# Context halves and three projection weights on one load queue, turned on TensorE in the order of landing, both context copies on VectorE

## The chip, the cores and the metric

One Trainium2 chip, of which the kernel uses one core. The metric is the device time of one execution in microseconds (us). Before the change three runs took 472.63, 471.83 and 472.56 us; the median is 472.56.

## What is computed

Eight sequences `x` of 512 tokens with 256 features are refined with a context of 64 rows per sequence. Cut to what matters:

```python
nx = layer_norm(x, ln_gamma, ln_beta)            # (8, 512, 256)
q = nx @ Wq
k, v = context @ Wk, context @ Wv                # context: (8, 64, 256)
weights = softmax(q @ k.T * 256 ** -0.5)
evidence = weights @ v
combined = concat([nx, evidence, broadcast(cond)])
router_probs = softmax(combined @ router_W + router_b)          # 3 experts
h = silu(combined @ e_w1 + e_b1)                                # 768 -> 512 per expert
routed = sum(router_probs * (h @ e_w2 + e_b2))
g = sigmoid(silu(combined @ gate_w1 + gate_b1) @ gate_w2 + gate_b2)
out = x + g * (routed @ out_w + out_b)
```

All of it is in float32.

## The kernel before, in words

The kernel has a setup stage and then a loop over four pairs of sequences (`NP = B // 2`, from L1138). In the loop the gate, the three experts and the outputs are computed with TensorE products of 128 x 128 weights by 128 x 512 tokens (`product`, L675). Setup and loop are written with `tc.manual_schedule(engines=None)`: each engine runs its instructions in the order in which the program lists them, and an instruction waits on semaphores for what it reads and for buffers that it overwrites. Nothing is planned by a cost model.

The change lies in the setup stage, in its first eight microseconds or so. That stage prepares what the attention needs from the context:

- *Loads.* L1078 to L1092 issue the large loads. The context is seen as 512 rows, in `NX = 4` tiles of 128 rows, and comes in two halves of 256 KB (`ctx_sb`, L1081). `Wk` and `Wq` (256 KB each, L1083) are issued by ScalarE (ACT). `Wv` (L1084), two sequences of x (512 KB each, `load_x`, L126) and the gate's and experts' first weights (`load_first`, `load_anchor`, L191 to L196) are issued by SyncE (SP). The queue that SP uses is called q1 in the profile, the one that ACT uses q10. GpSimd (POOL) issues small loads of bias rows (L172 to L179) in its own queue.
- *Wake products.* `wake(n)` (L250) lists n TensorE products of a tile of zeros with itself. Their result is never read.
- *Transposes.* The products with the context need it with features on the partitions. `context_transposes` (L271) takes a half at a time: four TensorE transposes of 128 x 128 into one PSUM bank, then one copy of 128 x 512 to `ctxT` in SBUF. The first half's copy is VectorE's (DVE), the second half's ScalarE's (L284). A `wake(1)` lies between the halves. `transpose_weights` (L286) does the same for a weight: four transposes into a bank and a copy on ScalarE (L293). It is called for Wk and for Wq.
- *Products.* `project` (L295) with Wv gives `vT` in two halves (`ps_v`, copied by ScalarE, L305), `join_keys` (L307) multiplies the turned Wk and Wq (`ps_kq`) so that keys and queries need one product, and `project` with that result gives `mr` (`ps_m`, copied by VectorE, L319).
- *PSUM banks.* `either` (L244) hands out four banks in turn for these steps.
- *The first two sequences.* `statistics` (L457) on VectorE computes mean and variance of each token of x as soon as x has landed; `deviation` (ScalarE), `normalize` (VectorE) and `transpose_x` (TensorE, copies on ScalarE and VectorE) follow, then `scores` and `softmax`.

The order on TensorE from the start is: 7 wake products, transposes of the first half, 1 wake product, transposes of the second half, of Wk, of Wq, half of the Wv products (`ps_v`), `join_keys`, the other half of Wv.

```python
        wake(7)
        context_transposes()
        transpose_weights(wkT, wk_sb, "wk")
        transpose_weights(wqT, wq_sb, "wq")
        statistics(0, 0, NT)
        deviation(0, 0)
        normalize(0)
        project(wv_sb, ctxT, keep_v, "v", (0,))
        join_keys()
```

Of the kernel before, what the change touches and what calls it, by code (L numbers as in the profile page):

```python
# [16 lines left out]
def kernel(  # L17
# [50 lines left out]
    nc = tc.nc  # L68
    P = 128
# [3 lines left out]
    KH = H // P  # L73
# [23 lines left out]
    def bank(i, name):  # L97
        return psum.tile([P, 512], F32, tag=f"b{i}", name=name)
# [4 lines left out]
    def misc(name):  # L103
        spare.append(spare.pop(0))
        return bank(spare[-1], name)
# [6 lines left out]
    ident = const.tile([P, P], F32, tag="ident", name="ident")  # L112
# [19 lines left out]
    def rows_of(w):  # L132
        return w.rearrange("(k p) n -> p k n", p=P)


    NX = B * CT // P
# [5 lines left out]
    def by_k(flat, n):  # L142
        return flat.rearrange("p (k n) -> p k n", n=n)

    scr = scratch(1, 2, "scr_ctx")
    ctx_sb, ctxT = by_k(scr[:, :HK], H), by_k(scr[:, HK:], B * CT)
    scr = scratch(1, 1, "scr_w")
    wk_sb, wq_sb, wqT, wv_sb = (by_k(scr[:, i * KH * H : (i + 1) * KH * H], H) for i in range(4))
# [95 lines left out]
    def either(name):  # L244
        turn[0] += 1
        return bank((1, 2, 0, 3)[turn[0] % 4], name)
# [3 lines left out]
    def wake(n):  # L250

        if not ps_wake:
            ps_wake.append(misc("ps_wake"))
        for _ in range(n):
            nc.tensor.matmul(ps_wake[0][:, :P], zeros, zeros, start=True, stop=True)  # L255
# [12 lines left out]
            condT[:, :, :B], pt[:, : KH * B].rearrange("p (k b) -> p k b", b=B)  # L268
        )

    def context_transposes():  # L271
        for d in range(2):
            if d:
                wake(1)
            pt = either(f"pt_ctx_{d}").rearrange("p (k c) -> p k c", k=KH)
            for k in range(KH):
                for t in range(NX // 2):
                    nc.tensor.transpose(
                        pt[:, k, t * P : (t + 1) * P],
                        ctx_sb[:, d * (NX // 2) + t, k * P : (k + 1) * P],  # L280
                        ident,
                    )
            half = slice(d * NX // 2 * P, (d + 1) * NX // 2 * P)
            (nc.scalar.copy if d else nc.vector.tensor_copy)(ctxT[:, :, half], pt)  # L284

    def transpose_weights(dst, w_sb, name):  # L286
        pt = either(f"pt_{name}")
        for k in range(KH):
            for i in range(KH):
                nc.tensor.transpose(  # L290
                    pt[:, k * H + i * P : k * H + (i + 1) * P], w_sb[:, i, k * P : (k + 1) * P], ident
                )
        nc.scalar.copy(dst.rearrange("p k n -> p (k n)"), pt)  # L293
# [163 lines left out]
    def statistics(b, t0, t1):  # L457
        j, i = b // 2, b % 2
        if b % 2 == 0 and t0 == 0:
            S["mv", j] = work.tile([P, 2, NT, nc.vector.BN_AGGR_DIM], F32, tag="mv", name=f"mv_{j}")  # L460
            S["sd", j] = work.tile([P, 2, NT], F32, tag="sd", name=f"sd_{j}")
        for t in range(t0, t1):
            st = work.tile([P, nc.vector.BN_STATS_DIM], F32, tag="st", name=f"st_{b}_{t}")
            nc.vector.bn_stats(st, x_sb[b][:, t, :])
            nc.vector.bn_aggr(S["mv", j][:, i, t, :], st)
# [610 lines left out]

    with tc.manual_schedule(engines=None):
        ctx_rows = context.flatten_outer_dims().rearrange("(t p) d -> p t d", p=P)  # L1078
        for d in range(2):
            half = slice(d * NX // 2, (d + 1) * NX // 2)  # L1080
            nc.sync.dma_start(ctx_sb[:, half, :], ctx_rows[:, half, :])  # L1081
        for w_sb, w in ((wk_sb, Wk), (wq_sb, Wq)):
            nc.scalar.dma_start(w_sb, rows_of(w))  # L1083
        nc.sync.dma_start(wv_sb, rows_of(Wv))  # L1084
        load_table(AF.Sqrt)
        load_x(0)
# [4 lines left out]
        for g in (1, 2):  # L1091
            load_first(g)  # L1092

        wake(7)
        context_transposes()
        transpose_weights(wkT, wk_sb, "wk")
        transpose_weights(wqT, wq_sb, "wq")
        statistics(0, 0, NT)
        deviation(0, 0)
# [148 lines left out]
```

## Time and profile before

| what | value |
|---|---|
| median of three runs | 472.56 us |
| the profiled execution, its own time | 472.56 us |
| span of the profiled execution, from first to last instruction | 470.4 us |
| TensorE (PE) busy | 465.1 us, 99% of the span |
| TensorE weight loads (PEld), overlapping PE | 221.1 us, 47% |
| VectorE (DVE) busy | 353.8 us, 75% |
| ScalarE (ACT) busy | 215.4 us, 46% |
| GpSimd (POOL) busy | 85.1 us, 18% |
| moved by the DMA engines | 36.84 MB, 78 GB/s over the span |

How to read it: the profile is one execution of the program, taken by the hardware profiler. Times count from the start of the span in microseconds. A group of instructions is named by its line in the kernel, its engine, its operation, and the tile that it writes and those that it reads (`out<-in`). PE's records overlap, since products are pipelined: a record's length is not what the product costs in a stream, the distance to the next record's start is. A wake product of float32 has two records, a transpose one. The chain of waits is followed back from the last instruction; in it each piece counts only what lies after the end of the piece before. For a load the profile gives the time from its issue to the landing of its last byte. "issue" in brackets is idle time for which the profile shows no other engine's work.

### The profile page before, as it was taken

The numbers are of one execution on the slowest core, as the hardware profiler recorded it, in microseconds if no ns is written. First come the engines' busy times: TensorE is split into PE (matmuls) and PEld (weight loads), VectorE is DVE, ScalarE is ACT, GpSimd is POOL, SyncE is SP. The second block draws the span as 40 slices with busy tenths as digits, with TensorE's granted clock in tenths as the row PEclk, the third lists the DMA queues.
The fourth block names the chain that finished last, engine by engine and source line by source line (L and its number), as shares of the span: only waits on it lengthen the run. The fifth ranks groups of instructions, "written<-read, shape, count | busy, mean of one in ns | idle before, by whom it ended". The sixth has DMA issues, their size and how long they took to land.

```text
span 470.4 us, 4664 instructions
## 1 busy us (share of the span) xinstructions
PE 465.1 (99%) x1439; PEld 221.1 (47%) x1439; DVE 353.8 (75%) x653; ACT 215.4 (46%) x388; POOL 85.1 (18%) x111
## 2 busy tenths in 40 slices
PE   9999999999999999999999999999999999999996
PEld 7744546445444444445454444445454444444454
DVE  3755847989989555889989555898989624797972
ACT  3455565657211647657311546658311465457000
POOL 5318123200062300000062300000052400000020
PEclk9999999999999999999999999999999999999999
DMA  9968330056232830442122740352122560000013
GB/s 288 376 108 179 57 136 0 0 117 90 36 67 32 171 135 0 91 88 45 17 47 44 162 152 1 75 106 45 18 45 45 84 186 0 1 0 1 0 22 68
DMA packets 126424, 36.84 MB, mean 78 GB/s; under 512 B 111548, under 2 KB 123392, under 8 KB 125888
## 3 DMA queue, kind: packets, MB, share of 16 engines
q1 hardware_dynamic: 122656, 28.59, 29.1%
q0 software_dynamic: 1856, 7.18, 4.8%
q10 hardware_dynamic: 1888, 0.79, 0.6%
q8 instruction: 11, 0.18, 0.2%
q14 instruction: 13, 0.11, 0.1%
HBM read 28.36 MB, written 8.18 MB: 78 GB/s over the span
## 4 chain that ended last, share of the span: by engine, by line
PE 91%; DVE 4%; SPq 3%; DMA 0%; issue 0%; ACT 0%; ACTq 0%
PE ps_u L677 40%; PE ps_z L677 17%; PE ps_y L677 14%; PE ps_vw L652 4%; SPq L392 3%; PE ps_gu L677 3%; PE ps_s L537 3%; PE ps_w2o L418 2%; PE ps_gz L677 1%; DVE h L951 1%; PE ps_wake L255 1%; DVE h L760 1%; PE ps_m L299 1%; PE ps_v L299 1%; PE ps_gy L677 1%; DVE r L960 0%
## 5 line engine op out<-in xcount | busy, mean ns | idle before, releaser
L760 DVE TENSOR_TENSOR h<-h,pb 128x512 f32<-128x512 f32 x96 | 61.9, 693 | 10.5 <-ACT h L710 10.5
L677 PE MATMUL ps_u<-h,w2o 128*128 128x512 f32 x144 | 63.9, 593 | 0.0
L677 PE MATMUL ps_u<-nxT,w 128*128 128x512 f32 x112 | 55.6, 607 | 0.0
L710 ACT ACTIVATE h<-h,abias 128x512 f32<-128x512 f32 x72 | 49.2, 718 | 8.8 <-DVE h L716 8.2
L677 PE MATMUL ps_z<-wT,vw 64*128 64x512 f32 x104 | 49.5, 605 | 0.0
L983 POOL TENSOR_TENSOR yb<-yb,xb 128x512 f32<-128x512 f32 x14 | 19.1, 1368 | 150.1 <-DVE yb L982 144.7
L677 PE MATMUL ps_z<-h,w2s 128*128 128x512 f32 x96 | 42.8, 595 | 0.2 <-DVE r L966 0.2
L719 ACT COPY h<-ps_u 128x512 f32<-128x512 f32 x48 | 27.9, 582 | 32.2 <-PE ps_u L677 31.9
L677 PEld LDWEIGHTS ps_u<-h,w2o 128*128 128x128 f32 x144 | 27.1, 190 | 31.3 <-issue 29.4
L716 DVE TENSOR_TENSOR h<-h,ps_y 128x512 f32<-128x512 f32 x24 | 16.4, 683 | 28.9 <-PE ps_y L677 25.0
L951 DVE TENSOR_TENSOR h<-h,h 128x1024 f32<-128x1024 f32 x24 | 34.3, 1483 | 0.0
L677 PEld LDWEIGHTS ps_u<-nxT,w 128*128 128x128 f32 x112 | 19.9, 189 | 29.8 <-issue 24.9
L710 ACT ACTIVATE h<-ps_u,abias 128x512 f32<-128x512 f32 x24 | 16.5, 687 | 30.2 <-PE ps_z L677 30.2
L677 PE MATMUL ps_y<-nxT,w 128*128 128x512 f32 x56 | 28.6, 592 | 0.0
L677 PE MATMUL ps_z<-T,ws 128*128 128x512 f32 x56 | 28.6, 592 | 0.0
L677 PEld LDWEIGHTS ps_z<-h,w2s 128*128 128x128 f32 x96 | 17.9, 190 | 22.1 <-issue 21.1
L677 PE MATMUL ps_u<-wT,vw 64*128 64x512 f32 x56 | 27.8, 611 | 0.0
L338 POOL DMA_DIRECT2D vrd<-vw x4 | 3.2, 802 | 132.5 <-ACT vw L659 132.5
L677 PE MATMUL ps_y<-wT,vw 64*128 64x512 f32 x56 | 27.0, 596 | 0.0
L652 PE MATMUL ps_vw<-w,vT 128*128 128x512 f32 (+1 forms) x64 | 26.9, 541 | 0.0
L677 PE MATMUL ps_u<-T,ws 128*128 128x512 f32 x56 | 26.7, 594 | 0.0
L677 PE MATMUL ps_z<-nxT,ws 128*128 128x512 f32 x56 | 26.6, 592 | 0.0
(209 smaller groups left out, 790.2 us busy)
## 6 DMA issues: line engine op xcount, KB each, us to landing
pb<-pd POOLq DMA_DIRECT2D x4, 1536.0 KB, 7.7
x<-in_x_dram SPq DMA_DIRECT2D x8, 512.0 KB, 5.4
xb<-in_x_dram SPq DMA_DIRECT2D x64, 64.0 KB, 2.4
out_dram<-yb SPq DMA_DIRECT2D x56, 64.0 KB, 2.0
w<-in_L_xcond_e_w_dram SPq DMA_DIRECT2D x6, 512.0 KB, 9.5
xd<-x SPq DMA_DIRECT2D x6, 512.0 KB, 2.9
xg<-xd SPq DMA_DIRECT2D x48, 64.0 KB, 2.4
scr_wa<-in_L_xcond_e_w_dram SPq DMA_DIRECT2D x3, 512.0 KB, 10.2
```

Source lines behind the costliest of these rows:

```text
L299: nc.tensor.matmul(ps, w_sb[:, k, m * P : (m + 1) * P], src[:, k, :], start=(k == 0), stop=(k == KH - 1))
L392: nc.sync.dma_start(dst[i * TB : (i + 1) * TB, k, :].rearrange("r (j c) -> r j c", c=TB), src[:, lo : lo + TB].rearrange("(j r) c -> r j c ...
L418: nc.tensor.matmul(ps[:, d * H : (d + 1) * H], w2T[:, k, (i + d) * P : (i + d + 1) * P], ow_sb[:, k, :], start=(k == 0), stop=(k == KH - 1),)
L537: nc.tensor.matmul(ps[:, t, :], nxT[:, k, t * P : (t + 1) * P], mr[:, k, b, :], start=(k == 0), stop=(k == KH - 1),)
L652: nc.tensor.matmul(ps, vT[:, k, j * 2 * CT : (j + 1) * 2 * CT], w1[:, KH + k, n0:n1], start=(k == 0), stop=(k == KH - 1),)
L677: nc.tensor.matmul(ps, lhsT, rhs, start=start, stop=True, skip_group_check=not start)
L710: nc.scalar.activation(h, h if src is None else src, AF.Silu, bias=abias[:, c, 2 * j + i : 2 * j + i + 1])
L716: nc.vector.tensor_tensor(h, h, part, ALU.add)
L719: nc.scalar.copy(chunk(n, i, d), part)
L760: nc.vector.tensor_tensor(h, h, S["pb", j][:, i, 2 * q // RC, :], ALU.mult)
L951: nc.vector.tensor_tensor(d, p, m, ALU.subtract)
L983: nc.gpsimd.tensor_tensor(yb, yb, S["xb", 2 * j + row][:, i, :], ALU.add)
```

## The change

The five loads of 256 KB go into SP's queue in the order first half, Wk, second half, Wq, Wv; ACT issues no load here. The function for the context's transposes takes one half at a time and its copy is always VectorE's. TensorE's order becomes: 5 wake products, first half, Wk, 1 wake product, second half, Wq, then the Wv products as before. All other code stays.

```diff
-    def context_transposes():
-        for d in range(2):
-            if d:
-                wake(1)
-            pt = either(f"pt_ctx_{d}").rearrange("p (k c) -> p k c", k=KH)
-            for k in range(KH):
-                for t in range(NX // 2):
-                    nc.tensor.transpose(
-                        pt[:, k, t * P : (t + 1) * P],
-                        ctx_sb[:, d * (NX // 2) + t, k * P : (k + 1) * P],
-                        ident,
-                    )
-            half = slice(d * NX // 2 * P, (d + 1) * NX // 2 * P)
-            (nc.scalar.copy if d else nc.vector.tensor_copy)(ctxT[:, :, half], pt)
+    def transpose_context(d):
+        pt = either(f"pt_ctx_{d}").rearrange("p (k c) -> p k c", k=KH)
+        for k in range(KH):
+            for t in range(NX // 2):
+                nc.tensor.transpose(
+                    pt[:, k, t * P : (t + 1) * P],
+                    ctx_sb[:, d * (NX // 2) + t, k * P : (k + 1) * P],
+                    ident,
+                )
+        nc.vector.tensor_copy(ctxT[:, :, d * NX // 2 * P : (d + 1) * NX // 2 * P], pt)
...
         ctx_rows = context.flatten_outer_dims().rearrange("(t p) d -> p t d", p=P)
-        for d in range(2):
-            half = slice(d * NX // 2, (d + 1) * NX // 2)
-            nc.sync.dma_start(ctx_sb[:, half, :], ctx_rows[:, half, :])
-        for w_sb, w in ((wk_sb, Wk), (wq_sb, Wq)):
-            nc.scalar.dma_start(w_sb, rows_of(w))
+        for d, w_sb, w in ((0, wk_sb, Wk), (1, wq_sb, Wq)):
+            part = slice(d * NX // 2, (d + 1) * NX // 2)
+            nc.sync.dma_start(ctx_sb[:, part, :], ctx_rows[:, part, :])
+            nc.sync.dma_start(w_sb, rows_of(w))
         nc.sync.dma_start(wv_sb, rows_of(Wv))
...
-        wake(7)
-        context_transposes()
+        wake(5)
+        transpose_context(0)
         transpose_weights(wkT, wk_sb, "wk")
+        wake(1)
+        transpose_context(1)
         transpose_weights(wqT, wq_sb, "wq")
```

## The prediction, made before the changed kernel ran

> **What bounds the kernel now.** I read the page's first part, then the chain of waits up to 26 us, the timeline engine by engine up to 20 us, the landings of the loads, and the waits of PE, DVE and SP.
>
> ```profile
> span 470.4 us, 4664 instructions
> ...
> PE 465.1 (99%) x1439; PEld 221.1 (47%) x1439; DVE 353.8 (75%) x653; ACT 215.4 (46%) x388; POOL 85.1 (18%) x111
> ```
>
> TensorE is busy for 465.1 of 470.4 us. Whatever shortens the way to the end must let TensorE start its necessary work sooner. All edits lie before the first product with Wv, `ps_v`; the chain shows the way there (start, length, what):
>
> ```profile
> 1.06 3.36 PE ps_wake L255 x14
> 4.41 0.03 issue
> 4.45 1.09 PE pt_ctx L278 x4
> 5.53 0.43 PE ps_wake L255 x2
> 5.96 0.96 PE pt_ctx L278 x4
> 6.93 0.57 PE pt_wk L290 x4
> 7.50 0.44 PE pt_wq L290 x4
> 7.94 1.72 PE ps_v L299 x4
> ```
>
> Two things are to be seen. Four transposes take 1.09 and 0.96 us, later 0.57 and 0.44: the timeline's single records start 0.21 us apart up to 6.93 and 0.11 us apart from 7.12, so TensorE doubles its speed at about 7.0. And the wake products are padding: a wake product is two records, 0.21 us each at the slow speed, and they fill time until a load lands. The last wake record starts at 3.99 and the first transpose at 4.45, so there TensorE waits some 0.25 us. The landings (issue to landing, last column) say for what:
>
> ```profile
> scr_ctx<-in_ctx_dram SPq DMA_DIRECT2D x1, 256.0 KB, 3.6
> scr_w<-in_L_xcond_Wk_dram ACTq DMA_DIRECT2D x1, 256.0 KB, 3.9
> ...
> scr_w<-in_L_xcond_Wv_dram SPq DMA_DIRECT2D x1, 256.0 KB, 5.1
> ...
> x<-in_x_dram SPq DMA_DIRECT2D x1, 512.0 KB, 6.1
> ```
>
> With the issue times of the timeline (0.74, 0.74, 1.74, 2.25): the first context half lands at 4.34, Wk at 4.64, Wv at 6.84, the first x at 8.35. By the same sum the second half (1.24 + 4.5) lands at 5.74, and its transposes start at 5.81; Wq at 1.28 + 4.9 = 6.18. TensorE is held by both context halves, not by Wk or Wq. The copies and what follows them:
>
> ```profile
> 6.96 0.59 ACT L284 COPY scr_ctx<-pt_ctx 128x512 f32<-128x512 f32 x1 [3.67 <-PE pt_ctx L278]
> ...
> 7.78 1.88 PE L299 MATMUL ps_v<-scr_ctx,scr_w 128*128 128x512 f32 x4
> ...
> 8.41 0.43 DVE L464 BATCH_NORM_STATS2 st<-x 128x6 f32<-128x256 f32 x1 [2.15 <-DMA x<-in_x_dram]
> ```
>
> The ScalarE copy ends at 7.55, before `ps_v` begins at 7.78 (record start; the chain counts it from 7.94, when the record before ends). VectorE is idle from 6.26 until x lands. From 7.94 to 23.49 TensorE has no gap in the chain, so a microsecond won or lost at `ps_v` is one at the end, if no load becomes late. From there:
>
> ```profile
> PE ps_w2o L418 <- DVE scr_w2T L410: 0.2, 1, 0.2
> PE ps_z L677 <- DVE r L966: 0.2, 1, 0.2
> PE ps_ar L356 <- ACT w L552: 0.2, 1, 0.2
> ```
>
> **What the Trainium skill says.** "DMA: Bandwidth & Descriptors", section "Issuing engines are not separate DMA queues": loads of different issuers share the same 16 engines, and a second issuer saves only issue time. The trace agrees: 373 GB/s at 3.25 to 3.5 us with two queues, 365 at 8.75 to 9.0 with one. Its section on queues, rings and completion order has the engines take turns between queues; agreed, from 3 to 5 us ACT's queue has 57.0% and SP's 51.3% of them. "TensorE: Matmul & The Clock Gate", Part 1: TensorE runs at half clock until it was busy through a window of about 3.4 us, which runs free of the kernel. The doubling at 7.0, 5.9 us after the first product, fits, and a moment that differs from run to run would explain 471.83 beside 472.56 and 472.63. Part 4 there says that transposes don't count as busy in the same way. This trace speaks against it: if the window that released the clock was about 3.6 to 7.0, it held only four wake records (0.85 us), and the one before twelve (2.5 us) and did not release it.
>
> **The change, part by part.**
>
> *Loads.* Five 256 KB loads in one queue, in the order of use, at about 0.5 us per issue (0.95 for two in the trace). Summing the trace's rates by quarter microseconds, 0.26 MB has moved by 3.2 us, 0.52 by 3.9, 0.79 by 4.6, 1.05 by 5.25, 1.31 by 6.05. A landing lags these marks by 0.47 us (first half and Wk together: 3.87, landed 4.34) to 0.8 (Wk 4.64, Wv 6.84). So the bounds are: first half 3.65 to 4.0, Wk 4.35 to 4.65, second half 5.05 to 5.4, Wq 5.7 to 6.05, Wv 6.5 to 6.85. I take 3.7, 4.5, 5.2, 5.95 and 6.75. The first half gains 0.6 us because Wk no longer shares its time; the total stays. The two issues come ahead of x and all weights on SP: x is issued at about 3.25 instead of 2.25. Cost nothing: its bytes start only after 1.31 MB have moved, at 6.05. If SP fell behind, x and VectorE's statistics would be late by as much. Later issues already wait for landings (SP waited 1.2 us for x at L192), not for SP. ACT loses two issues (1.0 us) that nothing waited for.
>
> *Two wake products fewer.* Minus four records of 0.213 = 0.85 us. They end at 3.35 instead of 4.2 (record starts plus spacing), and then TensorE waits for the first half until 3.8: 0.45 us idle.
>
> *Order of transposes.* First half from 3.8, four at 0.21: to 4.67. Wk has landed (4.5): four more to 5.52; one wake product to 5.95; second half, long landed, to 6.8, its last record ending at 6.59 + 0.42 = 7.0; Wq, partly at full clock, to 7.4. TensorE could issue `ps_v` at 7.4, 0.38 us sooner than 7.78.
>
> *Both copies on VectorE.* The second takes 0.69 us (the first half's row at 5.57) instead of 0.59, from 7.04 to 7.73, and its product follows 0.04 later: 7.77. This wait takes the place of the one removed: before, two weight transposes (8 records, 1.0 us) lay between the second half and `ps_v`, now one (0.6 us), and it doesn't cover the copy. Behind the copy on VectorE stand the statistics, which wait for x at 8.35: cover 0.6 us; a landing of x before 7.73 would be held. ACT's Wk copy moves from 7.54 to about 5.8 and its Wq copy from 8.02 to about 7.6; `join_keys` needs them at 9.66. Nothing.
>
> *Sum.* With the clock at 7.0: 7.78 - 7.77 = 0.0 us. With the clock at 5.0: before, the second half at 5.82 and twelve records of 0.11 give 7.1; after, Wv decides, 6.75 + 0.1 = 6.85. That is 0.93 us before this trace's 7.78: 472.56 - 0.93 = 471.63. With the clock at 5.6: wk slow, the rest fast, second half's transposes done at 6.35, copy to 7.07, `ps_v` 7.1: 471.88. A clock at 7.6 gives 7.77 to 7.85 again. The profiled execution took 472.56, its span 470.4 and 2.16 around it; it is the median run itself. Between 471.6 and 472.6, with either moment about as likely, I take **472.2**, 0.08% less.
>
> **The rivals.**
>
> *Likeliest: nothing measurable* (0.2%, 0.95 us, is about what a measurement of this kernel can tell from no change; 471.6 to 473.5). Chance 0.46.
>
> *Faster: Wv sets the pace early.* Where landings lag by 0.47, Wv is there at 6.5, and if the clock doubles before 5.5 nothing else holds `ps_v`: 6.6, 472.56 - 1.18 = 471.4. For it: the 471.83 run shows that the clock can be early. Against: two runs in three look late, and a late clock leaves VectorE's copy as the bound. Chance 0.34, as all these landing times are estimates with the room on the early side.
>
> *Slower: the clock comes a window later.* The idle 0.45 us ahead of the first half, up to 0.65 with a late landing and some 0.1 for Wk, leave a 3.4 us window that contains them 80 to 85% busy. The trace has one window of 75% that did not release the clock and one of 93% or more that did, so the limit lies between. If the release slips from 7.0 by 3.4 us to 10.4, the work from 7.8 to 10.4 runs at half speed and takes 1.3 us longer: 473.9. It is worth more than 0.2% from a release at about 9.7 on (1.9 us at half speed). Against: a window that starts after 3.8 has no gap and ends by 7.2. Chance 0.20.
>
> *The order is realised, but one queue fills the engines at half the rate at first.* First half at 4.0, everything 0.3 later: `ps_v` 8.05, 472.83. Inside "same".
>
> **How the numbers follow.** Faster 0.34, same 0.46, slower 0.20. The range goes from the faster case's lower end (471.2, Wv without any wait behind it) to within the slower case, 473.6; about one in ten lies beyond each. The likeliest case alone spans 471.6 to 472.9.
>
> **What would show it.** First-half transposes at 3.7 to 4.1; a gap before them; a VectorE copy of 0.69 us ending just before `ps_v`, which starts between 6.6 and 7.9; x landing at 8.35 within 0.3. Wrong would be: transposes still 0.21 apart after 8 us (clock), `ps_v` waiting for Wv after 7 (loads), statistics later than 8.7 (SP), or a difference that arises after 24 us.

## The result, and the profile after

| | before | after |
|---|---|---|
| median of 6 runs, us | 472.48 (471.83 to 472.63) | 473.76 (473.22 to 474.36) |
| profiled execution, us | 472.56 | 473.97 |
| its span, us | 470.4 | 471.8 |

The ratio after to before is 1.0033, interval 1.0023 to 1.0044: the change makes the kernel slower, by about 1.3 us or 0.3%. (The quotient of the two medians alone is 1.0027; the ratio is the estimate that comes with the interval.) The forecast was 472.2, "same".

The first lines of the page of after show no more than that TensorE still fills the span, with nearly the same busy time (464.9, before 465.1):

```profile
span 471.8 us, 4656 instructions
...
PE 464.9 (99%) x1435; PEld 220.3 (47%) x1435; DVE 355.9 (75%) x654; ACT 215.2 (46%) x387; POOL 85.4 (18%) x111
```

The span grew by 1.4 us while the busy time fell by 0.2, so TensorE stands idle longer (6.9 us of the span instead of 5.3). The waits of TensorE in after say where (engine, line, awaited step: us in total, times, longest):

```profile
PE ps_w2o L414 <- DVE scr_w2T L406: 1.0, 1, 1.0
PE ps_v L295 <- DMA scr_w<-in_L_xcond_Wv_dram: 0.5, 1, 0.5
```

Before, `ps_v` waited for no load, and `ps_w2o` waited 0.2. The first 12 us of the chain of waits of after (start, length, what) show the new holder of `ps_v`:

```profile
2.76 5.19 DMA scr_w<-in_L_xcond_Wv_dram
...
8.09 1.96 PE ps_v L295 x4
10.04 1.73 PE ps_kq L308 x8
```

Before, this stretch of the chain was all TensorE's own work. Now it is the load of Wv, which lands at 7.95 (predicted 6.75). The line of that load among after's DMA issues (last column: us from issue to landing) gives the same, 2.76 + 5.2; before it was 5.1 from 1.74:

```profile
scr_w<-in_L_xcond_Wv_dram SPq DMA_DIRECT2D x1, 256.0 KB, 5.2
```

The other landings, from issue and duration in the same way:

| lands at, us | before | predicted | after |
|---|---|---|---|
| first context half | 4.34 | 3.7 | 3.54 |
| Wk | 4.64 | 4.5 | 4.25 |
| second context half | 5.74 | 5.2 | 6.04 |
| Wq | 6.18 | 5.95 | 6.85 |
| Wv | 6.84 | 6.75 | 7.95 |
| first x | 8.35 | within 0.3 of 8.35 | 9.27 |

The first two loads are earlier than predicted and the rest later. The rate tells why. In the table of stretches the last column is what the DMA engines moved in that half microsecond, the one before it their busy share. First before, where the loads share SP's and ACT's queues:

```profile
3.50:4.00 0.50, 0.50 (x5) 0.50 (x3) 0.00 (x0) 0.00 (x0) 0.50 (x2) 1.00 1.10 383
...
5.00:5.50 0.50, 0.50 (x4) 0.50 (x3) 0.00 (x0) 0.00 (x0) 0.50 (x2) 1.00 1.07 341
```

And the same stretches of after, with one queue:

```profile
3.50:4.00 0.50, 0.33 (x3) 0.30 (x3) 0.00 (x0) 0.00 (x0) 0.50 (x2) 1.00 1.00 338
...
5.00:5.50 0.50, 0.50 (x5) 0.50 (x4) 0.50 (x1) 0.00 (x0) 0.50 (x2) 1.00 0.51 134
5.50:6.00 0.50, 0.50 (x3) 0.30 (x2) 0.04 (x1) 0.29 (x1) 0.50 (x2) 1.00 0.58 168
```

Between 5 and 6 us the DMA engines are half idle (0.51, 0.58) though Wv and x still stand in the queue. Over the ten half microseconds from 3 to 8 us before moved 1.82 MB and after 1.39 MB. At some 360 GB/s the missing 0.43 MB are 1.2 us. After had moved 0.1 MB more ahead of 3 us (116 GB/s from 0.5 to 3 us, before 78), which is 0.3 us; that leaves some 0.9 us. By the start of the statistics that wait for it (9.26, before 8.41), x is 0.85 us late.

Following the chains of both kernels down, after is behind by 0.38 us at the end of the first `ps_v` products (10.04, before 9.66), by 0.29 at `ps_ar` (26.05, before 25.76), and by 1.08 at the first `ps_w2o` (53.99, before 52.91). It is still 1.08 behind at the last output copy (467.99, before 466.91); the remaining 0.3 us lies in the final stores. So in this execution the larger part of the loss arises far from the loads. VectorE's records of after near 43 us:

```profile
43.21 0.94 DVE L591 TENSOR_TENSOR pv<-w,vr 128x384 f32<-128x384 f32 x1
44.19 0.55 DVE L597 TENSOR_REDUCE le<-pv 128x6 f32<-128x384 f32 x1
44.77 0.97 DVE L591 TENSOR_TENSOR pv<-w,vr 128x384 f32<-128x384 f32 x1
...
46.66 0.38 DVE L601 TENSOR_TENSOR lg<-le,lg 128x12 f32<-128x12 f32 x1
```

The same instructions of before:

```profile
42.91 0.83 DVE L595 TENSOR_TENSOR pv<-w,vr 128x384 f32<-128x384 f32 x1
43.78 0.55 DVE L601 TENSOR_REDUCE le<-pv 128x6 f32<-128x384 f32 x1
44.37 0.64 DVE L595 TENSOR_TENSOR pv<-w,vr 128x384 f32<-128x384 f32 x1
...
45.80 0.17 DVE L605 TENSOR_TENSOR lg<-le,lg 128x12 f32<-128x12 f32 x1
```

The products of two SBUF tiles are longer by 0.11 + 0.33 + 0.21 us in these lines, and a further one (`lg` with the bias, 0.37 after 0.25) by 0.12, together 0.77 us; the reduction between them, of one tile, is the same 0.55. That is about the growth from 0.29 to 1.08. Beside them GpSimd adds its own tiles (`combine_weights`), which end at 45.7 before and 47.4 after, because the load that opens them starts later. That load waits for the store of the router's rows (`vrd`), which was issued 0.85 us later (24.38, before 23.53; GpSimd's work ahead of it follows x) and took 11.4 us instead of 10.5 beside the weights. GpSimd's lines of after and then of before:

```profile
36.07 0.56 POOL L336 DMA_DIRECT2D vr<-vrd  x1 [10.88 <-DMA scr_w<-in_L_xcond_e_w_dram]
...
43.70 1.04 POOL L204 TENSOR_TENSOR w<-w 128x256 f32<-128x256 f32 x1
```

```profile
34.36 0.56 POOL L340 DMA_DIRECT2D vr<-vrd  x1 [10.02 <-DMA vrd<-vw]
```

The Trainium skill's page "SBUF — State Buffer", section "Who interferes with whom", says that a VectorE instruction with two SBUF inputs contends with a GpSimd instruction that reads SBUF. This trace agrees: `pv` takes 0.55 us alone (later in the same trace) and 0.94 and 0.97 here, and the GpSimd add at 43.70 takes 1.04 instead of 0.72.

The 0.3 us at the very end are a separate thing. The last store is on its way for longer, and SyncE waits longer for it. First before, then after:

```profile
out_dram<-y ACTq DMA_DIRECT2D x1, 64.0 KB, 2.2
SPq L1243 <- DMA out_dram<-y: 0.2, 1, 0.2
```

```profile
out_dram<-y ACTq DMA_DIRECT2D x1, 64.0 KB, 2.5
SPq L1240 <- DMA out_dram<-y: 0.7, 1, 0.7
```

This goes with the queues and not with late loads. In the seven profiles, of those below too, in which ACT issues no early load, the span ends 4.16 to 4.63 us after the start of TensorE's last instruction; in the seven in which ACT issues some it ends 3.82 to 3.87 us after it, also where x is late. A single transfer of 8 KB in a further queue (q14) falls 1.8 to 1.9 us after that instruction in the first seven, amid the last stores, and 1.1 to 1.3 us after it in the others. That it holds the stores up is not shown; no run tests it.

In what follows, the moment at which TensorE's clock doubles is taken from the trace's own record of it (7.08 before, 6.50 after); the column of the granted clock above reads 1.00 throughout and doesn't show it, but the spacing of the transposes does. That moment differs between executions that start alike: before, b_pool_late and b_pool_early give TensorE the same work up to there, and the clock doubles at 7.08, 5.24 and 6.48, with `ps_v` at 7.78, 7.06 and 7.43. So some tenths of a microsecond at `ps_v` between two single profiles can come from the clock alone.

### The profile page after: what moved, and what is told of

Same layout as the page of the kernel before. It is cut to its first block, busy times and chain, and to the rows that moved or that the text cites. A ratio compares the mean times of both kernels' runs of the same rounds, so it can differ in the third digit from the quotient of the medians.

```text
span 471.8 us, 4656 instructions
## 1 busy us (share of the span) xinstructions
PE 464.9 (99%) x1435; PEld 220.3 (47%) x1435; DVE 355.9 (75%) x654; ACT 215.2 (46%) x387; POOL 85.4 (18%) x111
## 4 chain that ended last, share of the span: by engine, by line
PE 91%; DVE 6%; DMA 1%; issue 0%; SPq 0%; ACT 0%; DVEq 0%; ACTq 0%
PE ps_u L673 41%; PE ps_z L673 18%; PE ps_y L673 14%; PE ps_vw L648 4%; PE ps_gu L673 3%; PE ps_s L533 3%; PE ps_w2o L414 2%; PE ps_gz L673 1%; DVE h L947 1%; DMA scr_w<-in_L_xcond_Wv_dram 1%; PE ps_v L295 1%; DVE h L756 1%; PE ps_m L295 1%; PE ps_gy L673 1%; DVE pv L591 1%
## 5 line engine op out<-in xcount | busy, mean ns | idle before, releaser
L756 DVE TENSOR_TENSOR h<-h,pb 128x512 f32<-128x512 f32 x96 | 62.0, 696 | 10.5 <-ACT h L706 10.5
L673 PE MATMUL ps_u<-T,w 128*128 128x512 f32 x56 | 26.6, 592 | 0.0
```

The source lines that it names most:

```text
L673: nc.tensor.matmul(ps, lhsT, rhs, start=start, stop=True, skip_group_check=not start)
L756: nc.vector.tensor_tensor(h, h, S["pb", j][:, i, 2 * q // RC, :], ALU.mult)
```

## The experiments

Each ratio is to runs of before made together with the run, whose median lay between 471.74 and 472.41; so ratios can be compared with each other, and times less well.

Theories: **loads** (one queue delivers late, and what follows the loads pays), **wake** (two wake products fewer delay the clock), **copy** (VectorE's second copy holds `ps_v`), **collision** (GpSimd beside VectorE near 43 us carries the cost).

### One part at a time

**b_one_queue**: before, with only the order and the queue of the loads changed; seven wake products and ScalarE's copy stay.

```diff
-        for d in range(2):
-            half = slice(d * NX // 2, (d + 1) * NX // 2)
-            nc.sync.dma_start(ctx_sb[:, half, :], ctx_rows[:, half, :])
-        for w_sb, w in ((wk_sb, Wk), (wq_sb, Wq)):
-            nc.scalar.dma_start(w_sb, rows_of(w))
+        for d, w_sb, w in ((0, wk_sb, Wk), (1, wq_sb, Wq)):
+            part = slice(d * NX // 2, (d + 1) * NX // 2)
+            nc.sync.dma_start(ctx_sb[:, part, :], ctx_rows[:, part, :])
+            nc.sync.dma_start(w_sb, rows_of(w))
```

> The kernel before with only its loads changed: all five in SP's queue, first half, Wk, second half, Wq, Wv. 7 + 1 wake products, the order of transposes and ScalarE's copy of the second half stay. Theory (one queue): Wv lands at 7.7 to 8.2, x at 9.0 to 9.4, time 473.4 to 474.0. Rivals 1 and 2 (copy, wake products): 472.3 to 472.7, no change.

Measured: 473.72 us, ratio 1.0034 (1.0021 to 1.0048): as much as the whole change. Its stretches show the same low rates, earlier and longer:

```profile
3.50:4.00 0.50, 0.50 (x5) 0.50 (x4) 0.00 (x0) 0.00 (x0) 0.50 (x2) 1.00 0.83 258
...
4.50:5.00 0.50, 0.50 (x4) 0.50 (x3) 0.00 (x0) 0.00 (x0) 0.50 (x2) 1.00 0.78 231
```

Its chain of waits shows what that costs here:

```profile
1.75 5.11 DMA scr_ctx<-in_ctx_dram
...
8.03 0.85 PE pt_wk L290 x4
...
9.73 2.08 PE ps_v L299 x4
```

The second half lands at 6.86, and all transposes after it still take 0.85 us for four, not 0.44: TensorE stood still for 1.22 us, and the clock doubles only at 10.34. `ps_w2o` comes at 54.78 without a wait, and `pv` takes 0.71 and 0.56. So the edit of the queue alone gives the loss, in this execution by another route than in after. (It was the slowest of its five, 474.74; the others took 473.12 to 474.57.)

**a_act_queue**: after, with only the loads of Wk and Wq back on ACT's queue.

```diff
-            nc.sync.dma_start(w_sb, rows_of(w))
+            nc.scalar.dma_start(w_sb, rows_of(w))
```

> The changed kernel with only the loads of Wk and Wq given back to ScalarE's queue; order of transposes, 5 + 1 wake products and both copies on VectorE stay. Theory (one queue): the five loads in a single queue move too slowly between 4.5 and 7 us (some 110 to 300 GB/s in the changed kernel), so Wv lands at 7.95 instead of 6.84, and all that is behind it about 0.9 us later; with two queues the rate should stay at 350 or more, Wv land at 6.7 to 7.0, x at 8.3 to 8.5, and the time be 472.2 to 472.7. Rival 1 (VectorE's copy is the wait): nothing of that is touched, ps_v stays at 8.0 or later, time 473.5 to 473.9. Rival 2 (two wake products fewer leave the clock slow for longer): time 473.5 to 473.9 as well.

Measured: 473.60, ratio 1.0029 (1.0019 to 1.0039). The dip is gone (348 to 383 GB/s in all stretches from 3 to 8 us), but the time doesn't come back. The waits of TensorE:

```profile
PE pt_ctx L275 <- DMA scr_ctx<-in_ctx_dram: 0.7, 1, 0.7
PE ps_v L295 <- DVE scr_ctx L280: 0.3, 1, 0.3
```

With two queues the first half lands at 4.09, which five wake products don't reach (they end at 3.35), and VectorE's copy now holds `ps_v`. The profiled execution was the fastest of its eight (472.81, clock at 7.19), so it doesn't show what the slower seven did. That a missing queue dip leaves a loss of the same size means that something else in the change costs too; the next runs look for it in the wake products.

**b_wake5**: before, with five wake products instead of seven. **a_act_queue_w7**: a_act_queue, with seven. In both the edit is this line, in the second the other way round.

```diff
-        wake(7)
+        wake(5)
```

> The kernel before with wake(5) in place of wake(7) and nothing else. TensorE then stands still from 3.35 us until the first half is turned at 4.4, about 1.0 us. Theory (clock): a window of 3.4 us that contains this pause doesn't release the clock, so in most executions full speed comes at 7.6 to 10.8 us instead of 4.5 to 7.9, and the median rises by 0.7 to 1.5 us, to 472.8 to 473.6. Rival (wake products are padding, the wait for the load hides them): 471.8 to 472.5, as before.

> The changed kernel with Wk and Wq on ScalarE's queue and wake(7) in place of wake(5). Theory (clock): the run with wake(5) and two queues was slow, 473.6, because TensorE paused some 0.7 to 0.9 us ahead of the first half; with the pause filled the time is 472.0 to 472.6. Rival (the order of the transposes or VectorE's copy costs it): 473.3 to 473.7.

Measured: b_wake5 473.64, ratio 1.0020 (1.0012 to 1.0028). a_act_queue_w7 472.78, ratio 1.0006 (0.9998 to 1.0014). The chain of b_wake5:

```profile
4.52 1.09 PE pt_ctx L278 x4
...
7.82 0.85 PE pt_wq L290 x4
8.67 1.85 PE ps_v L299 x4
```

TensorE pauses for 0.96 us ahead of the first half (by the end of the last wake record), and the transposes after 7 us still go at half speed, 0.85 us for four: the clock doubles at 8.82 instead of 7.08. The two wake products were thus no padding to be saved: with two queues they cost 0.2% when left out, and with them back in a_act_queue 0.23 points of its 0.29 come back. What stays there, 0.06%, is not told from none; the new order of transposes and VectorE's copy, which holds `ps_v` for 0.35 us in it, cost 0.14% at most, the upper end of the interval. The time itself lies a little above what was expected.

**a_act_copy**: after, with the second half's copy on ScalarE again.

```diff
-        nc.vector.tensor_copy(ctxT[:, :, d * NX // 2 * P : (d + 1) * NX // 2 * P], pt)
+        (nc.scalar.copy if d else nc.vector.tensor_copy)(ctxT[:, :, d * NX // 2 * P : (d + 1) * NX // 2 * P], pt)
```

> The changed kernel with the second half's copy given back to ScalarE; one load queue stays. Theory (one queue): Wv lands after either copy, so nothing changes, 473.5 to 474.0. Rival 1 (the copy is the wait): ps_v starts some 0.1 to 0.4 us sooner and the time falls to 473.3 or less.

Measured: 473.53, ratio 1.0032 (1.0020 to 1.0043). The copy is not what costs in after; there VectorE's ended at 7.63, ahead of Wv at 7.95. Rates fall again, to 203 at 6.0 to 6.5 us, and the second half lands at 6.50.

**a_more_wake**: after, with the pauses filled.

```diff
-        wake(5)
+        wake(7)
         transpose_context(0)
         transpose_weights(wkT, wk_sb, "wk")
-        wake(1)
+        wake(3)
         transpose_context(1)
+        wake(2)
         transpose_weights(wqT, wq_sb, "wq")
```

> The changed kernel, single queue and both copies on VectorE, with more wake products in the places where TensorE waited: 7 at the start, 3 ahead of the second half, 2 ahead of Wq. If the clock is the whole cause: 471.9 to 472.6. If the slow loads of the single queue are the whole cause: 473.4 to 474.0, since Wv still lands at 7.8 to 8.2 and x at 9.2 or later. If it is both: 472.7 to 473.3.

Measured: 473.64, ratio 1.0025 (1.0015 to 1.0035). In its profile the clock doubles at 5.73, TensorE has no pause up to 20 us, and `ps_v` starts at 7.88, earlier than in after. Still `ps_w2o` waits 1.0 us and starts at 53.84; `pv` takes 0.98 twice. So in this run an early clock didn't mend the one queue, and the collision near 43 us became the suspect. Two reservations: Wv has landed at 7.35 here, so what holds `ps_v` until 7.88 is the filling itself, which is more than the pauses needed; and the profiled execution (474.25) was the slowest of nine, with the longest end of all, 4.63 us after TensorE's last instruction starts.

### The collision

**b_pool_late**: before, with about 1.7 us of adds put ahead of GpSimd's first `combine_weights`, on a tile that is overwritten afterwards, so that the result is unchanged. **b_pool_early**, **a_pool_early** and **a_wake_pool**: before, after and a_more_wake, with all three `combine_weights` moved ahead of GpSimd's wait for the router's rows, where GpSimd is idle for some 10 us.

```diff
+    nc.gpsimd.memset(gw2s, 0.0)
...
+        for n in (3, 2):
+            nc.gpsimd.tensor_tensor(gw2s[:, :n, :], gw2s[:, :n, :], gw2s[:, :n, :], ALU.add)
         combine_weights(0)
```

```diff
-    def spread_router_rows(j):
+    def spread_router_rows(j, between=None):
         vrd = dram.tile([E, 2 * CT], F32, tag="vrd", name=f"vrd_{j}")
         nc.gpsimd.dma_start(vrd.rearrange("e c -> c e"), S["vw", j][:, R0:])
+        if j == 0 and between is not None:
+            between()
...
-        spread_router_rows(0)
+        spread_router_rows(0, lambda: [combine_weights(g) for g in range(E)])
...
-        combine_weights(0)
...
-        combine_weights(1)
-        combine_weights(2)
```

> The kernel before with GpSimd given about 1.7 us of additional work (two tensor additions on a scratch tile, results not used) just before combine_weights(0), so that its weight combinations end at about 47.4 instead of 45.7 us, as in the changed kernel. Theory (second part: VectorE's router_logits runs slower while GpSimd works, and TensorE waits for it at ps_w2o): TensorE's start is as before, its wait at ps_w2o grows from 0.2 to about 1.0 us, time 473.1 to 473.5, with the first two products pv at 0.9 us or more instead of 0.83 and 0.64. Rival (VectorE was slow there because loads or the vr tile came late): time 472.3 to 472.7, pv as before.

> The kernel before with GpSimd's combinations of the experts' weights issued ahead of the load of vr on GpSimd (they then run at 24 to 34 us instead of 35 to 43.3), so that they no longer lie beside VectorE's router_logits. Theory (VectorE slows down beside GpSimd, and TensorE waits for it at ps_w2o): the wait there of 0.2 us in the profile, and more in executions whose clock is released early, goes; the first two pv take 0.55 to 0.65 us; time 471.4 to 472.0. Rival (the wait at ps_w2o doesn't matter, or GpSimd's work collides with something else): 472.1 or more.

> The changed kernel with nothing else changed than GpSimd's combinations ahead of the load of vr. The wait at ps_w2o should go; what is left is the clock and the late Wv. If the collision is most of the loss: 472.4 to 472.9. If the clock (5 wake products) is most of it: 473.3 to 473.8.

> The changed kernel, single queue and both copies on VectorE, with the wake products of a_more_wake (7, 3 and 2) and with GpSimd's combinations of the experts' weights ahead of the load of vr. In a_more_wake the clock came in time (5.7 us), ps_v started at 7.88, and the time was still 473.64, with a wait of 1.0 us at ps_w2o. Theory (the single queue costs through VectorE's router_logits, which meets GpSimd's late combinations): the wait at ps_w2o is gone and the time falls to 472.2 to 472.8. Rival (the single queue costs through the late loads themselves): 473.4 to 473.8.

| run | us | ratio (interval) | clock at | `ps_v` at | `pv`, us | first `ps_w2o` at |
|---|---|---|---|---|---|---|
| b_pool_late | 472.37 | 1.0007 (0.9999 to 1.0015) | 5.24 | 7.06 | 1.04, 1.07 | 53.06, after a wait of 1.0 |
| b_pool_early | 472.07 | 0.9992 (0.9984 to 1.0000) | 6.48 | 7.43 | 0.52, 0.56 | 53.23 |
| a_pool_early | 473.49 | 1.0036 (1.0022 to 1.0050) | 4.59 | 7.55 | 0.52, 0.56 | 53.51 |
| a_wake_pool | 473.71 | 1.0039 (1.0026 to 1.0051) | 6.67 | 8.32 | 0.51, 0.56 | 53.99 |

The collision near 43 us is real and movable: `pv` goes from 1.07 to 0.52 with the place of GpSimd's work. But a late collision by itself costs little: b_pool_late has `pv` at 1.04 and 1.07 and a wait of 1.0 at `ps_w2o`, as after has, and its ratio is 1.0007, at most 1.0015. With the adds moved early the change still costs 1.0036, and with the pauses filled as well 1.0039. So both forecasts of a cure missed. These two are not a clean removal, though: the adds now lie beside VectorE's softmax. There the same product takes, in b_pool_early and then in before:

```profile
24.64 0.83 DVE L564 TENSOR_TENSOR w<-w,rs 128x256 f32<-128x256 f32 x1
```

```profile
24.38 0.43 DVE L562 TENSOR_TENSOR w<-w,rs 128x256 f32<-128x256 f32 x1
```

and from `ps_ar` (25 us) to 36 us TensorE loses 0.8 us against before in b_pool_early, 0.6 in a_wake_pool and 0.2 in a_pool_early. The waits of a_pool_early show what else stands in the way:

```profile
PE pt_ctx L275 <- DMA scr_ctx<-in_ctx_dram: 0.6, 1, 0.6
PE ps_rb L324 <- DVE condT L267: 0.5, 1, 0.5
```

With the clock at 4.59, the earliest of all runs, TensorE waits for the second half and then for VectorE, whose statistics stand behind an x that lands at 9.43. b_pool_late shows the reverse: its clock doubles at 5.24, long before the edit acts, its `ps_v` is 0.72 us earlier than before's, and the wait at `ps_w2o` takes all of it back (53.06, before 52.91).

### What makes one queue slow

**a_x_act**: after, with the first two loads of x on ACT's queue, so that two queues are at work though the five loads stay in one. **a_small_late**: after, with three fills of a scratch tile ahead of GpSimd's small loads (of 1 to 9 KB), to move these out of the way. Each time here is of one execution, without an interval.

```diff
-        nc.sync.dma_start(x_sb[b], x[b].rearrange("(t p) d -> p t d", p=P))
+        (nc.sync if b > 1 else nc.scalar).dma_start(x_sb[b], x[b].rearrange("(t p) d -> p t d", p=P))
```

```diff
+    for _ in range(3):
+        nc.gpsimd.memset(scr[:, 1024:], 0.0)
```

> The changed kernel with the two loads of x issued by ScalarE, the five loads of context and weights still in SP's queue. Looked at for its load rate only. Theory (one queue cannot keep the rate up in this stretch, any second queue can): 340 GB/s or more from 3.5 to 7 us, and no dip. Rival (the dip comes with the order or the issue times of the five loads on SP): a dip below 300 GB/s between 4 and 7 us as in the three runs with one queue.

> The changed kernel with three fills of 128 x 1024 of an unused part of a scratch tile ahead of GpSimd's small loads, which delays those by some 2 to 4 us. Looked at for its load rate; the time is not comparable, as the bias rows arrive late. Theory (one queue): the dip below 300 GB/s between 4 and 7 us stays. Rival (the dip is GpSimd's small loads mixing in): it moves with them or goes.

Measured: a_x_act 475.81. The engines are full again from 3.5 us on (346 to 387 GB/s, one stretch of 281), so the memory and the engines could deliver; but x takes its share, Wk lands at 5.85, the second half at 8.34, Wv at 9.95, TensorE pauses twice for about 1 us and the clock doubles at 12.07. a_small_late 473.62: the dip stays, in another place (244 at 3.5 to 4.0, then this):

```profile
6.00:6.50 0.50, 0.50 (x4) 0.38 (x2) 0.00 (x0) 0.13 (x1) 0.50 (x2) 1.00 0.86 205
```

GpSimd's queue moves nothing before 5.5 us here, so the small loads are not needed for a dip. Whether they deepen it after 5.5 us, where they now run, is not settled.

## Why the prediction was wrong

**The failed step is the one on loads.** It summed the rates of the trace of before and said "the total stays". Those rates were those of two queues. Every profile with the five loads and x in one queue (seven: after, b_one_queue, a_act_copy, a_more_wake, a_wake_pool, a_pool_early, a_small_late) falls below 300 GB/s somewhere between 3.5 and 7 us, with a lowest half microsecond of 134 to 231. So Wv landed at 7.95 instead of 6.75, and x 0.85 us late. Of the six that share the five loads between two queues (before, b_wake5, b_pool_late, b_pool_early, a_act_queue, a_act_queue_w7), five have no half microsecond below 341, and b_pool_early has one, of 284. b_one_queue gives a loss of the whole size (1.0034) by the edit of the queue alone. The prediction leaned on the 365 GB/s at 8.75 to 9.0, where one queue was at work, and carried it to a queue that has all the loads from the start, without a trace of that. The Trainium skill's "DMA: Bandwidth & Descriptors", section "Issuing engines are not separate DMA queues", says that a second issuer saves only issue time. From 3.5 to 7 us here the measurements say otherwise, and they decide. Why one queue dips stays open. In before SP's queue is alone from about 6 us and moves 354 to 367 GB/s up to 8 us, so neither the time nor a lone queue as such explains it. The records show single packets of 1 KB that take up to 1.02 us (the median is 0.046) but not what held them.

The rival "one queue fills the engines at half the rate at first" had the right suspect in the wrong place and at the wrong size. The start is faster (first half at 3.54, not 4.0) and the dip comes afterwards; that its `ps_v` at 8.05 is close to the measured 8.09 is luck.

**The sum.** It asked only when `ps_v` starts. The start moved by 0.31 us (7.78 to 8.09) against a predicted 7.77 at the late clock, and `ps_v` waited for Wv, the sign that was named as showing the loads wrong. It then took a difference at `ps_v` as the difference at the end, "if no load becomes late". x did become late, by 0.85 us, 0.77 us more arose at 43 to 47 us, past the 24 us that the prediction had named as the limit, and 0.33 us after TensorE's last instruction. The step fails for gains too. In before TensorE already waits 0.2 us for VectorE at `ps_w2o`, which the prediction showed and gave no term; so VectorE sets that moment. a_act_queue_w7 starts `ps_v` at 7.46 (before 7.78), yet `ps_w2o`, after a wait of 0.6 us, at 53.14 (before 52.91); its profiled execution took 472.70, before's 472.56. So even with the loads in time the 0.93 us of the sum are not to be expected whole at the end. The runs show no fixed path for the loss. Late loads show at the clock (b_one_queue), at `ps_v` (after), at the statistics (a_pool_early, a_act_copy with 0.3) or beside GpSimd (after, a_more_wake), and the longer end of the span comes with each of these runs. That closing one path opens another is an inference from single profiles (in a_wake_pool and a_more_wake the filling holds `ps_v`); measured is that the ratio stays between 1.0025 and 1.0039.

**Two wake products fewer.** The 0.45 us of pause became 0.38, since the first half came early. The slower rival was right as a mechanism: a pause can cost a clock window. b_wake5 shows it, at 0.2%, with a pause of 1.17 counted in the same way (3.35 to 4.52). Its forecast of 473.9 lies close to the measured 473.76, but that doesn't confirm it: in the profiled execution of after the clock doubles at 6.50, earlier than before's 7.08. For the other five runs of after the moment isn't known. In after the five wake products fit the early first half; without the one queue they don't. The two edits cost 0.34% and 0.20% alone and 0.33% together (0.23 to 0.44); the sum, 0.54%, lies above that, so they don't add.

**Copies.** The prediction had VectorE's copy end at 7.73 and hold `ps_v`. It ended at 7.63 and held nothing, because Wv came later. Where the loads are in time it does hold `ps_v` (0.34 us in a_act_queue). The step was right for the landings that it assumed.

**The faster case** needed Wv at 6.5 and an early clock. The clock was early in a_pool_early (4.59) and a_more_wake (5.73), and Wv wasn't there: it landed at 7.41 and 7.35.

No version clearly beats before. Nearest is b_pool_early, 0.9992 with an interval up to 1.0000: it clears the collision at 43 us, but its softmax now runs beside GpSimd's adds, and TensorE waits 0.6 us at `ps_ar`.

## What to carry to other kernels

A rate read while two queues feed the DMA engines is not the rate of one queue, and a stretch in which one queue works alone later is not the rate of a queue that carries everything from the start. Before loads are merged into one queue, price the merge with the rate kept and with the rate lost, or run it alone. Padding ahead of a clock change is fitted to the moment at which the loads land, so the two are changed together and tested apart. A gain or a delay at one point of the chain is not the same at the end while another engine has little slack on the way: give the short waits of the chain a term. And if removing the wait that the profile names gives nothing back, look where the removed work went before you call the wait harmless.

## What the runs showed of the hardware beyond the prediction

- One queue of rows of 1 KB moved less than 300 GB/s, down to 134, for 2 to 3.5 us early in the kernel, where two queues moved 341 to 387 but for one half microsecond.
- The stretches of full clock in the 14 profiles last 460.80, 464.21 or 467.63 us, so they differ in steps of 3.41 us. Of the windows of that length that end with the doubling, the least busy by TensorE's records was 87% (a_act_queue, 3.77 to 7.19); after's (3.09 to 6.50) was 95%. Of those a step or two earlier, which did not double it, the busiest was 82% (a_x_act, 1.83 to 5.25); before's (0.25 to 3.67) was 76%, b_wake5's (1.99 to 5.40) 72% and b_one_queue's (3.52 to 6.93) 64%. So in these traces the limit lies between 82 and 87%. Transposes of float32 filled most of before's window (3.67 to 7.08) and of after's, so here they count.
- VectorE's product of two SBUF tiles of 128x384 took 0.52 to 0.56 us alone and up to 1.07 beside GpSimd's adds; one of these adds took 1.04 instead of 0.72. The softmax product of 128x256 took 0.83 instead of 0.43.
- The span ended 4.16 to 4.63 us after the start of TensorE's last instruction where ACT's queue had carried no early load, and 3.82 to 3.87 us where it had, seven profiles each.
